# Four graph layers on one core: counts read in long runs, attention weights put ahead of their pieces, last rows stored bank by bank

## The chip, the cores and the metric

The kernel runs on one core of a Trainium2 chip. A core has TensorE (PE, matmuls and transposes), VectorE (DVE), ScalarE (ACT), GpSimd (POOL) and SyncE (SP); each works through its own list of instructions in order and waits for the others by semaphores. SP, POOL and ACT also issue DMAs. The metric is the device time of one execution in microseconds; the time before is the median of five runs.

## The reference

The input is a table of 3327 nodes with 512 features and an adjacency matrix of zeros and ones. Four layers follow one another, each as `x = layernorm(x + layer(x, adj))`:

```python
# layers 0, 2, 3: graph attention with 8, 8 and 4 heads
e = leaky_relu(f1[:, None] + f2[None, :])         # one number per pair of nodes and head
attention = softmax(where(adj > 0, e, -9e15))     # over the neighbours
h = attention @ (x @ W)                           # layers 2 and 3: elu of it
# layer 1: mean over the first 64 neighbours
keep = adj & (cumsum(adj, axis=1) <= 64)
cnt = keep.sum(axis=1)
xj = leaky_relu(((keep @ x) / max(cnt, 1)) @ W_nb.T + b_nb)
xi = leaky_relu(x @ W_line.T + b_line)
out = xi + where(cnt > 0, xj, 0)
```

## The kernel before

The nodes are padded to 26 tiles of 128 rows (`NT`), and a row of 512 floats is 2 KB. The mask is kept on the chip for the whole run, with one byte for each pair of nodes. Half of the nodes (`HALF`, 13 tiles) is attended to at a time.

**An attention layer** (`Layer`) first projects every tile: `project1` transposes a tile by four PE transposes into `pt`, ACT copies it to `xT` (L260), and `project2` makes two banks `pw` from it (L269), from which ACT takes the head columns `rc`, `qc`, `dc` (L270, L273) and DVE the values `vt` (L275). `prepare` turns the columns of one half into rows by PE transposes `pr` and ACT copies `rr` (L310, L312), and into scale and bias columns on DVE (L316 to L320). `cut` splits columns into bf16 pieces `pc` and copies them into `sden` and `sm`, the stationary operands of the denominators (L333 to L349). `attention` then runs two halves times four slices (`unit`). In each slice, for every source tile j, DVE makes the weights `t` (L403, 128x1664), ACT makes the corrections `y` from them (L406), and PE multiplies `t` with the values into `po` (L426); `den` adds the denominators in `pd` three tiles later (L378). Work of other kinds is put between the tiles as `jobs`, one after each tile.

After a slice, `transposed` (L454) brings the result back to rows by quads of tiles (`QUADS`: 4, 4, 4 and 1), and it is stored to `hd`. The denominators of the second half's last slice go through DRAM: `dd` is stored by one DMA (L505), and `place` (L515) reads it back as `pes` by 16 DMAs. These are held as `late` and run inside the next stage, at its loop's tiles 4 (`place`, on SP) and 8 (`finish_sums`, on DVE).

**Finishing a layer** (`finish_steps`) is done tile by tile inside the next stage's projection: load `h` and the residual `xr` (L126), divide by the denominators on DVE (L181), for layers with elu an exp on ACT (L186) and two additions on DVE (L192, L193), otherwise one (L195), and the layer norm (`norm_rows`: statistics on DVE L152, L153, a square root on ACT L154, reciprocal and shift on DVE L155, L158, the scaling on ACT L161). Loads of `h` go by SP or POOL, those of `xr` by POOL.

**The neighbour mean** (`sage`) projects each tile twice (`pz` L722, `pi` L725) and then sums over the kept neighbours (`acc` L845). The counts `cnt` of each node come from `ctd`, a DRAM tensor whose row 26 holds one count for each node. They are read by one DMA into `cb` (128 partitions, 26 columns, one bf16 element at a time: `"o (t p) -> p (o t)"`) and turned into three columns at the loop's tile 8.

**The third stage** (`third`) finishes layer 2 and projects layer 3. Its loop loads groups of two tiles ahead (`load_group`), and runs the steps of the group after the current one between the current tile's two projection steps.

**The tail.** Layer 3's first half is finished and stored inside the attention to the second (`later`). The second half stays in `g` on the chip; its last slice is finished by `final` after the last matmul: a division (L999), an exp (L1002), two additions (L1004, L1005) and statistics (L1008, L1009), for each quad in turn. Then the tiles are scaled in two groups, of 8 and 5 tiles, and stored, even tiles by SP and odd ones by POOL (`store`).

**What sets the order.** PE's list follows the program text (`manual_schedule`). The other engines' lists are made by a scheduler, which orders instructions by its own estimate of when each can run; `tc.keep_in_program_order(ins)` pins one instruction to its place in the program. So an edit can change the order of instructions around it, on DVE, ACT and SP alike, that the diff does not name. Tile pools with a number of buffers (`bufs`) make an instruction wait until a buffer's last reader is done.

## Time and profile before

| what | value |
|---|---|
| median of five runs | 3388.35 us (3386.66 to 3393.47) |
| the profiled execution's own time | 3390.44 us |
| its span, from the first instruction to the last | 3388.7 us |
| granted TensorE clock | 0.984 of full |
| instructions | 47192 |
| bytes moved by DMA | 284.29 MB, 84 GB/s on average |

The stages lie as follows in the trace: layer 0 until 958 us; the neighbour mean's projection 960 to 1170 and its sums to 1765; the second attention (layer 2) 1768 to 2556; the third stage's projection 2557 to 2696; the attention of layer 3 to 3359; the tail to 3388.7.

A line of the timeline gives the start, the time in us, the engine, the line in the kernel, the operation, output and inputs with their shapes, the number of instructions put together, and in brackets the time that the engine sat idle before it and what ended this. An "SPq" or "POOL" line with DMA_DIRECT2D is the issue of a transfer, not the transfer. The chain of waits is followed back from the last instruction, at each step to what released it.

### The profile page before, as it was taken

The numbers are of one execution on the slowest core, as the hardware profiler recorded it, in microseconds if no ns is written. First come the engines' busy times: TensorE is split into PE (matmuls) and PEld (weight loads), VectorE is DVE, ScalarE is ACT, GpSimd is POOL, SyncE is SP. The second block draws the span as 40 slices with busy tenths as digits, with TensorE's granted clock in tenths as the row PEclk, the third lists the DMA queues.
The fourth block names the chain that finished last, engine by engine and source line by source line (L and its number), as shares of the span: only waits on it lengthen the run. The fifth ranks groups of instructions, "written<-read, shape, count | busy, mean of one in ns | idle before, by whom it ended". The sixth has DMA issues, their size and how long they took to land.

```text
span 3388.7 us, 47192 instructions
## 1 busy us (share of the span) xinstructions
PE 3253.3 (96%) x18475; PEld 1626.1 (48%) x18475; DVE 2684.2 (79%) x2615; ACT 2357.0 (70%) x2142; POOL 241.7 (7%) x390
## 2 busy tenths in 40 slices
PE   8899999999979999999989999999998999999997
PEld 6634344444434445545544444444446754445443
DVE  5799999999967544444449999999998766668886
ACT  2398998999953333333338999999997755558985
POOL 3100000000010011111110000000002000010110
PEclk9999999999989999999999999999999999999998
DMA  9644111110143343333320111111117411122311
GB/s 369 221 128 124 49 49 40 57 45 28 44 122 122 115 128 85 88 84 87 82 77 19 48 50 48 50 50 42 38 33 234 159 41 42 41 51 78 97 42 49
DMA packets 288055, 284.29 MB, mean 84 GB/s; under 512 B 107533, under 2 KB 223575, under 8 KB 287832
## 3 DMA queue, kind: packets, MB, share of 16 engines
q1 hardware_dynamic: 254024, 170.61, 16.7%
q0 software_dynamic: 28288, 102.97, 9.6%
q10 hardware_dynamic: 5520, 7.69, 0.7%
q8 instruction: 146, 2.39, 0.3%
q14 instruction: 77, 0.63, 0.1%
HBM read 212.01 MB, written 69.17 MB: 83 GB/s over the span
## 4 chain that ended last, share of the span: by engine, by line
PE 83%; DVE 5%; DMA 5%; issue 4%; ACT 3%; POOL 0%; SPq 0%; ACTq 0%; POOLq 0%; DVEq 0%
PE po L426 49%; PE acc L845 12%; PE pd L378 7%; PE pw L269 5%; DVE t L403 3%; PE pz L722 3%; PE pi L725 3%; DMA raw<-in_adjT_dram 2%; ACT y L406 1%; PE pk L805 1%; PE pt L454 1%; DMA asb<-in_a_dram 0%; DMA r<-rr 0%; PE pa L1066 0%; PE pt L259 0%
## 5 line engine op out<-in xcount | busy, mean ns | idle before, releaser
L403 DVE SCALAR_TENSOR_TENSOR t<-rb,qc,mask 128x1664 f32<-128x1664 f32 x1040 | 1958.8, 1943 | 168.1 <-PE po L426 148.0
L406 ACT ACTIVATE y<-t,bi,sc 128x1664 fp8e4<-128x1664 f32 x1040 | 1769.5, 1765 | 309.9 <-PE pd L378 291.4
L426 PE MATMUL po<-t,vj 128*64 128x448 f32 (+3 forms) x8320 | 1909.8, 520 | 24.4 <-DVE t L403 24.1
L426 PEld LDWEIGHTS po<-t,vj 128*64 128x64 f32 (+1 forms) x8320 | 837.4, 148 | 974.5 <-issue 706.7
L845 PE MATMUL acc<-zs,kt 128*128 128x512 bf16 x1352 | 402.1, 381 | 0.0
L845 PEld LDWEIGHTS <-kt 128*128 128x128 fp8e4 x2002 | 196.5, 98 | 242.1 <-issue 8.4
L269 PE MATMUL pw<-wsb,xT 128*128 128x264 f32 (+1 forms) x1248 | 300.4, 396 | 12.3 <-DVE vt L275 10.0
L797 ACT CAST pk<-cy 128x512 f32<-128x512 bf16 x169 | 99.1, 588 | 278.0 <-DVE kt L809 268.1
L378 PE MATMUL pd<-y,sden 128*32 128x448 fp8e4 (+1 forms) x4160 | 259.3, 341 | 10.4 <-ACT y L406 10.4
L269 PEld LDWEIGHTS pw<-wsb,xT 128*128 128x128 f32 x1248 | 240.4, 196 | 57.0 <-ACT xT L260 10.4
L845 PE MATMUL acc<-zl,kt 128*128 128x512 bf16 x650 | 246.9, 380 | 0.0
L378 PEld LDWEIGHTS <-sden 128*32 128x32 bf16 x4160 | 117.3, 96 | 162.6 <-issue 139.8
L809 DVE SCALAR_TENSOR_TENSOR kt<-pk,mask 128x512 fp8e4<-128x512 f32 x169 | 116.0, 687 | 95.5 <-PE pk L805 95.5
L275 DVE TENSOR_TENSOR vt<-pw,dc 128x256 f32<-128x256 f32 x156 | 59.1, 417 | 150.6 <-ACT dc L270 144.8
L357 POOL DMA_DIRECT2D rb<-r x40 | 21.3, 532 | 1686.7 <-DVE t L403 1663.8
L273 ACT COPY rc<-pw 128x8 f32<-128x8 f32 (+1 forms) x78 | 12.7, 163 | 156.3 <-PE pw L269 156.3
L817 DVE SCALAR_TENSOR_TENSOR y<-acc,cnt,bnb 128x512 f32<-128x512 f32 x26 | 19.5, 750 | 97.5 <-PE acc L845 90.0
L690 POOL DMA_DIRECT2D cy<-ctd x91 | 67.9, 747 | 386.3 <-ACT pk L797 312.5
L722 PE MATMUL pz<-wn,xT 128*128 128x512 f32 x208 | 94.7, 598 | 0.4 <-ACT xT L716 0.4
L725 PE MATMUL pi<-wl,xT 128*128 128x512 f32 x208 | 93.5, 592 | 0.0
L154 ACT ACT_TABLE_LOAD x46 | 59.0, 1283 | 37.0 <-DVE mv L153 36.4
L624 DVE TENSOR_SCALAR mask<-raw 128x832 fp8e4<-128x832 int32 (+2 forms) x90 | 53.7, 604 | 38.8 <-DMA raw<-in_adjT_dram 38.6
(185 smaller groups left out, 1702.2 us busy)
## 6 DMA issues: line engine op xcount, KB each, us to landing
vj<-v SPq DMA_DIRECT2D x312, 128.0 KB
rb<-r POOLq DMA_DIRECT2D x40, 832.0 KB, 4.7
raw<-in_adjT_dram SPq DMA_DIRECT2D x67, 416.0 KB
cy<-ctd POOLq DMA_DIRECT2D x78, 256.0 KB, 4.0
h<-hd SPq DMA_DIRECT2D x61, 256.0 KB
v<-vt SPq DMA_DIRECT2D x50, 256.0 KB
hd<-hb SPq DMA_DIRECT2D x48, 256.0 KB
xr<-x POOLq DMA_DIRECT2D x45, 256.0 KB, 3.2
```

The lines of the kernel that those rows point to most:

```text
L269: nc.tensor.matmul(pw[e][:, :FW + H], xT[:, c, :], wsb[:, c, e, :], start=c == 0, stop=c == FC - 1)
L275: nc.vector.tensor_tensor(vt[:, hs, :], pw[e][:, :FW].rearrange("p (h d) -> p h d", d=D), self.dc[:, t, hs].rearrange("p (h e) -> p h e", e=1)
L378: nc.tensor.matmul(pd[c][32 * kk:32 * kk + 32, :w_], lhsT, rhs, start=(kk, c) not in seen, skip_group_check=final is not None, stop=last a ...
L403: nc.vector.scalar_tensor_tensor(t, rb[k], self.qc[:, j, h:h + 1], mask[:, j, i0:i0 + IW], op0=ALU.max, op1=ALU.mult)
L406: nc.scalar.activation(y, t, AF.Sigmoid, bias=self.bi[:, j, h:h + 1], scale=self.sc[:, j, h:h + 1], saturate=False)
L426: nc.tensor.matmul(po[c][k * D:(k + 1) * D, :z - a_], vj[:, j % 2, k * D:(k + 1) * D], ts[k][:, a_:z], start=j == 0, stop=j == NT - 1)
L690: nc.gpsimd.dma_start(out=cy[:, :n, :], in_=ctd[t:t + n, b * GW:(b + 1) * GW] .rearrange("(o t) i -> o t i", o=1).to_broadcast([P, n, GW]))
L722: nc.tensor.matmul(pz, xT[:, c, :], wn[:, c, :], start=c == 0, stop=c == FC - 1)
L725: nc.tensor.matmul(pi, xT[:, c, :], wl[:, c, :], start=c == 0, stop=c == FC - 1)
L797: nc.scalar.copy(pks[k % 2], carry[b, t // 4 * 4][:, t % 4:t % 4 + 2, :])
L809: nc.vector.scalar_tensor_tensor(kt, pk, NEIGHBOURS, mask[:, t:t + 2, i0:i0 + GW], op0=ALU.is_le, op1=ALU.mult, saturate=False)
L845: nc.tensor.matmul(acc, kts[t][:, s * P:(s + 1) * P], zs(t, c) if c < 2 else zl[:, t, :], start=t == 0 and c == 0, stop=t == NT - 1 and c ...
```

## The change

There are five edits, in three places of the program and two helpers that they share.

1. Counts. The row of counts is loaded as 26 rows of 128 elements (`cr`, by SP), copied to float by ACT (`cf`), transposed by PE at the loop's tile 8, and the three `cnt` operations read it from PSUM. The first of them is no longer pinned.
2. `place` pins the first of its 16 loads to its place in the program, where it runs in the next stage (layers 0 and 2).
3. `finish_steps` can pin the exp of a group's first tile; `load_group` asks for this for the group of tiles 2 and 3.
4. Second attention. `cut` of the first half moves from before the attention into its jobs, as the second one, with its first copy pinned. `prepare` and `cut` of the second half come two jobs later.
5. Tail. In the last slice all quads are divided first (quad k+2 is transposed after quad k is divided), with buffers of their own for the last two. Then come the four exps, and for each quad two additions, statistics and the square root, after which the quad before it is scaled and stored. All these are pinned in this order.

```diff
@@ finish_steps
+            pinned=False
             if layer.elu:
                 e = pool.tile([P, F], F32, name="e", bufs=ebufs)
-                nc.scalar.activation(e, h, AF.Exp)
+                ins = nc.scalar.activation(e, h, AF.Exp)
+                if pinned and s == 0:
+                    tc.keep_in_program_order(ins)
@@ place
                         for m in range(4):
-                            eng.dma_start(out=pes[...], in_=src[m])
+                            ins = eng.dma_start(out=pes[...], in_=src[m])
+                            if end and kk + m == 0:
+                                tc.keep_in_program_order(ins)
@@ unit, final
             take = []
-            return [lambda: take.append(transposed(*QUADS[0])), lambda: take.append(transposed(*QUADS[1])),
-                    sums, reciprocals] + [lambda q=q: take[q]() for q in range(2)] + \
-                [lambda q=q: transposed(*q)() for q in QUADS[2:]]
+            def step(k):
+                if k < len(QUADS):
+                    take.append(transposed(*QUADS[k]))
+            jobs = [lambda: step(0), lambda: step(1), sums, reciprocals]
+            for k in range(len(QUADS)):
+                jobs += [lambda k=k: take[k](), lambda k=k: step(k + 2)]
+            return jobs
@@ sage
-                cb = zp.tile([P, NT], BF, name="cb")
-                nc.gpsimd.dma_start(out=cb, in_=ctd[NT:NT + 1, :].rearrange("o (t p) -> p (o t)", p=P))
+                cr = fp.tile([NT, P], BF, name="cr", bufs=1)
+                nc.sync.dma_start(out=cr, in_=ctd[NT:NT + 1, :].rearrange("o (t p) -> (o t) p", p=P))
...
                     if t0 == 8:
-                        tc.keep_in_program_order(
-                            nc.vector.tensor_scalar(cnt[:, 0, :], cb, NEIGHBOURS, 1.0, op0=ALU.min, op1=ALU.max))
+                        cf = fp.tile([NT, P], F32, name="cf", bufs=1)
+                        nc.scalar.copy(cf, cr)
+                        pt = ps.tile([P, FC, P], F32, name="pt")
+                        cb = pt[:, 0, :NT]
+                        nc.tensor.transpose(cb, cf, ident[:NT, :NT])
+                        nc.vector.tensor_scalar(cnt[:, 0, :], cb, NEIGHBOURS, 1.0, op0=ALU.min, op1=ALU.max)
@@ third, load_group
-                        groups.append(finish_steps(fp, x2, L2, t0, 2, 10, nc.gpsimd if t0 < 4 else nc.sync, 6))
+                        groups.append(finish_steps(fp, x2, L2, t0, 2, 10, nc.gpsimd if t0 < 4 else nc.sync, 6,
+                                                    pinned=t0 == 2))
@@ third, final (divide, exp, add1, add2 are the former take() cut into functions)
+                def scale(q0, n):
+                    qs = slice(q0, q0 + n)
+                    keep(nc.vector.reciprocal(rs[:, qs, 0], rs[:, qs, 0]))
+                    keep(nc.vector.scalar_tensor_tensor(rs[:, qs, 1], mv[:, qs, 0], -1.0, rs[:, qs, 0], ...))
+                    for q in range(q0, q0 + n):
+                        y = g[:, q, :]
+                        if q % 4 == 3:
+                            keep(nc.scalar.activation(y, y, AF.Identity, bias=rs[:, q, 1:2], scale=rs[:, q, 0:1]))
+                        else:
+                            keep(nc.vector.tensor_scalar(y, y, rs[:, q, 0:1], rs[:, q, 1:2], ...))
+                        store(y, HALF + q, q)
+                for _, _, exp, _, _ in lasts:
+                    keep(exp())
+                for k, (q0, n, _, add1, add2) in enumerate(lasts):
+                    keep(add1())
+                    keep(add2())
+                    for q in range(q0, q0 + n):
+                        keep(nc.vector.bn_stats(out=st[:, q, 1, :], in_=g[:, q, FB:]))
+                        keep(nc.vector.bn_aggr(out=mv[:, q, :], in_=st[:, q, :, :]))
+                    keep(nc.scalar.activation(rs[:, q0:q0 + n, 0], mv[:, q0:q0 + n, 1], AF.Sqrt, bias=eps))
+                    if k > 0:
+                        scale(*lasts[k - 1][:2])
+                scale(*lasts[-1][:2])
@@ second attention
-                L2.cut(mp, 0, "pc", 1)
-                L2.attention(rp, lambda pool, half, s: [lambda: None] * 2 +
-                             [lambda: L2.prepare(mp, 1, "rr", 1, True), lambda: L2.cut(mp, 1, "pc", 1, True)]
+                L2.attention(rp, lambda pool, half, s: [lambda: None, lambda: L2.cut(mp, 0, "pc", 1, True)] +
+                             [lambda: None] * 2 + [lambda: L2.prepare(mp, 1, "rr", 1, True), lambda: L2.cut(mp, 1, "pc", 1, True)]
                              if (half, s) == (0, 0) else [],
```

## The prediction

> **What bounds the kernel now.** I read the page's busy shares and the shares of the chain of waits first, then the chain and the timelines of the four places that the change touches.
>
> ```profile
> PE 3253.3 (96%) x18475; PEld 1626.1 (48%) x18475; DVE 2684.2 (79%) x2615; ACT 2357.0 (70%) x2142; POOL 241.7 (7%) x390
> PE 83%; DVE 5%; DMA 5%; issue 4%; ACT 3%; POOL 0%; SPq 0%; ACTq 0%; POOLq 0%; DVEq 0%
> ```
>
> TensorE is busy 96% of the span: there is little to win outside its few gaps, and everything that only moves work beside it is free. One gap is where the neighbour mean starts (chain first, then the timelines of DVE and PE):
>
> ```profile
> 960.99 9.09 DMA dd<-red
> ...
> 979.46 3.19 DMA pes<-dd
> 968.56 0.18 DVE L753 TENSOR_SCALAR cnt<-cb 128x26 f32<-128x26 bf16 x1 [7.60 <-DMA cb<-ctd]
> 974.22 0.69 DVE L195 TENSOR_TENSOR h<-h,xr 128x512 f32<-128x512 f32 x1 [4.25 <-DMA xr<-in_x_dram]
> 980.87 0.69 DVE L181 TENSOR_TENSOR h<-h,rec 128x512 f32<-128x512 f32 x1 [3.23 <-DMA h<-hd]
> 986.31 1.12 PE L714 MATMUL pt<-ident,h 128*128 128x128 f32 x4 [17.00 <-ACT h L161]
> ```
>
> PE waits 17.00 us for tile 2, whose finish hangs on DVE, which waits in order for three loads. After it PE's timeline shows no wait until 1170, so what is won here stays won. The second attention is the opposite case; its start on PE, and a stretch of it by engine (length; PE, PEld, DVE, ACT and POOL busy; clock; DMA):
>
> ```profile
> 1770.11 1.06 PE L426 MATMUL po<-t,vj 128*64 128x448 f32 x2 [4.29 <-DVE t L403]
> 1773.84 10.48 PE L426 MATMUL po<-t,vj 128*64 128x448 f32 x46 [2.67 <-DVE t L403]
> 1968.00:2168.00 200.00, 199.12 (x1424) 93.66 (x1422) 200.00 (x108) 187.27 (x128) 2.65 (x5) 1.00 0.15 49
> ```
>
> DVE has 200.00 of 200 us there, so DVE sets its end. The third projection is mixed; its waits on DVE and PE:
>
> ```profile
> 2567.47 0.69 DVE L181 TENSOR_TENSOR h<-h,rec 128x512 f32<-128x512 f32 x1 [3.75 <-DMA h<-hd]
> 2575.91 1.12 PE L259 MATMUL pt<-ident,h 128*128 128x128 f32 x4 [6.63 <-ACT h L161]
> 2587.34 0.66 PE L259 MATMUL pt<-ident,h 128*128 128x128 f32 x4 [1.42 <-ACT h L161]
> 2637.81 1.23 PE L310 MATMUL pr<-ident,rc 128*4 128x128 f32 x5 [2.87 <-ACT rr L312]
> ```
>
> The tail after the last matmul is DVE, then transfers at full rate (last line, a window):
>
> ```profile
> 3365.80 1.29 DVE L1004 SCALAR_TENSOR_TENSOR g<-e,g 128x512 f32<-128x512 f32 x2
> 3368.72 0.24 DVE L1008 BATCH_NORM_STATS2 st<-g 128x6 f32<-128x128 f32 x1
> 3368.87 0.19 DVE L1009 BATCH_NORM_AGGREGATE mv<-st 128x2 f32<-128x12 f32 x1
> 3375.57 2.62 SPq L133 DMA_DIRECT2D out_dram<-g  x4
> 3378.16 1.92 DVE L1028 TENSOR_SCALAR g<-g,rs 128x512 f32<-128x512 f32 x4
> 3378.00:3386.00 8.00, 0.00 (x0) 0.00 (x0) 2.04 (x5) 0.81 (x1) 1.90 (x4) 0.50 1.01 353
> ```
>
> The profiled run took 3390.44 us (span 3388.7, 1.74 around it), 2.1 above the median 3388.35 and inside the runs' 3386.66 to 3393.47. I take the sum of differences from its rows and set it on the median.
>
> **A, the counts.** Removed: the load cb (POOL, 1.49 us to issue, 10.1 to landing) and DVE's wait for it. Added: cr, one SP issue (SP's loads take 0.32 to 0.5); a 26-column ACT copy (some 0.25 us) that stands before zs, where ACT waits anyway; one transpose (a group of four takes 1.12 us cold, 0.44 warm: 0.11); and cnt's reads from PSUM while PE is the bound. The wait of 7.60 by itself is worth only 0.7: behind it DVE waits for h until 969.27 and for xr until 974.22. What counts is the transfer. Windows of 2 us give 367 GB/s at 960 to 962, then 190 and 151 while cb's element-sized packets run: 682 of some 1440 KB, so 2.1 us are lost to all transfers. The store before xr and dd lie in that backlog, so both may come 2.1 earlier. SP then puts h(4) behind six pes issues instead of eight: 2 x 0.645 = 1.3. Against it, in the compiled order DVE adds tile 3 and the first projected rows after h(4)'s divide and not before, so h(4) to the last step of rs takes 5.7 us (nine passes of 0.6 and three short ones) and not 4.34: +1.4. Together -2.1 +1.4 -1.3 +0.1 = -1.9; tile 2's add is up to 0.6 sooner too, and I take **-2.2**. Ends: 0, if the 1 MB load of wl gates xr and not cb; -4, if both 2.1 and 1.3 count and DVE's 1.4 hides in a wait.
>
> **B, the second attention.** The first four t (1.864 us each, start to start) now precede the 19 cut operations, which took 1763.25 to 1768.13. PE's first product comes some 4 us earlier, but DVE has the same work and no idle time after, so it ends when it did. What is saved: operations that wait for their predecessor start 0.035 us after its end, others 0.08 before it; ten such waits x 0.115 = 1.2, some of which stay between neighbours: **-0.5**. Ends: -1.2; +0.3, if a t waits for its rows (rb 4.7 to landing, loaded long before). PE's transposes for the second half move two tiles later, under PE's own slack.
>
> **The third projection.** The edit is one pin on one exp, and a pin on the first of 16 pes issues, but the scheduler reorders DVE, ACT and SP. ACT now scales tiles 0 and 1 before the exp table load and the exp: first transposes 1.5 us earlier, worth nothing, because pw is in order and tile 2 is late. On DVE the work between the wait that ends at 2567.47 and rs of tile 2 was 7.4 us; now tiles 5 and 6 are divided first and tiles 4 and 5 added: 14 passes of 0.61, two halves of 0.33 and four short ones, 9.6: **+2.2** at the 6.63 wait. Tile 4 is then ready early, so the wait of 1.42 at 2587.34 goes: **-1.4**. At prepare, between the pr transposes and the copy that frees their bank, ACT has two table loads where it had one (1.28), and a sqrt, a dc and a wait for DVE in place of an exp: **+1.7** on the 2.87. Sum **+2.5**. Behind the moved DVE divide of tile 10 stand tile 7's add and a bank-freeing vt; its load is still behind the pes issues on SP (16 x 0.645), issued near 2582.5 and landing near 2586, when PE wants that bank at 2588.5: just hidden. Ends: -1.5 (only the stall that goes); +5.2, if 2.7 of that load are exposed.
> The Trainium skill, "ScalarE: Activation LUTs", What ACT_TABLE_LOAD costs, gives 1.28 us plus 1.38 us of drain for each switch. Here the load at 2633.85 is followed by exp at 2635.15, 1.30 later; no drain shows, and by the page the sum would be 1.4 higher.
>
> **C, the tail.** All four divides come first (the third waits for its transposes, about +0.65), then bank by bank add, add, statistics, with each step waiting for the one before. Rows: two adds of different banks start 0.605 apart; a dependent one would be 0.69 + 0.035 = 0.725. Statistics and aggregate interleaved cost 0.264 a tile (3368.72 to 3368.98), dependent 0.275 + 0.11 = 0.385. So +0.85 over the adds, +1.56 over 13 tiles, +0.82 for two more reciprocal and rs pairs, less 0.5 of waits for exp: DVE ends 3.4 later, at 3383.5. The first rows go out at 3374.1 instead of 3375.55, but after four of them DVE is away on bank 2 until 3378.9. Nine of 13 tiles, 2.36 MB, remain from about 3379.4 at 353 GB/s: 6.7 us, to 3386.1 against 3386.3. **-0.1**. Ends: -2.5, if dependent steps start as soon as independent ones do (0.605, 0.264), for then DVE keeps up and the transfers run unbroken from 3377; +1.5, if the last tile's two issues (0.73 each, after 3383.5) come last.
> The Trainium skill, "VectorE: DVE Perf Modes", The DRAIN you can't avoid, says that a semaphore between chained DVE operations costs nothing extra. By it C would be -2.5. The rows 3363.70, 3363.92 and 3364.14 (operations of 0.18, 0.216 apart, each waiting) against 0.605 for 0.69 speak against it.
>
> Sum: -2.2 - 0.5 + 2.5 - 0.1 = -0.3, so 3388.35 - 0.3 = **3388.0** (the profiled run's counterpart 3390.1).
>
> **The rivals.** Faster: the tail's transfers are what ends it, and they run unbroken: C at -2.5, and with A at -4 and B at -1.2 the third projection must give back under 1 to pass -6.8. For it speaks that DMA is the last thing running; against it the 0.605 and 0.725. Time 3381.0.
> Slower: the load of tile 10 that DVE waits for in order. Its neighbours took 2.9 to 8.5 us to landing; at 8.5 it lands at 2591, PE's bank comes 5 late and all of it lies on the path: -0.3 + 5 = 3393. It makes the change slower than before from 0.3 us of exposure on, and slower than can be told from no change from 7.
> The change doesn't do it: cb is not what delays xr and dd, since wl and blb (1.25 MB) are in the same backlog. Then A is 0 and the time 3390.2.
>
> **How the numbers follow.** This kernel can tell 0.2% (6.8 us) from no change. Likeliest case 0.52 (3384 to 3392), no gain from A 0.15, faster rival 0.19, slower 0.14. Past -6.8 lie 0.16 of the faster rival and 0.03 of the likeliest case: 0.19. Of the slower one 0.12 lies past +6.8, since the tail's +1.5 and A's 0 may join. The range 3380.5 to 3394.0 takes in both rivals' times and leaves out 2 in 10.
>
> **What would show it.** A: no wait for cb, xr's wait ending near 972, PE's 17.00 wait near 14.8. B: first t near 1764 on the old clock, and the attention still ending about where it did. Third projection: the first long PE wait longer than 6.63, the next one gone, a second table load before rr, and DVE waiting for h just before tile 7's add. C: statistics 0.385 apart, DVE's last operation later than before, a gap in the stores after the first four. I am wrong if DVE's waits there are not 0.035 behind the predecessor's end, if the reordered third projection costs more than 5, or if the earlier xr does not come.

## The result and the profile after

The changed kernel takes 3389.69 us (median of 26 runs, 3384.80 to 3397.24). The kernel before, run beside it on the same chips, takes 3392.85 us (44 runs, 3386.54 to 3399.02). The ratio is 0.9993, with a 95% interval of 0.9988 to 0.9998: 2.4 us less, between 4.1 and 0.7. By the bound of 0.2% that is no change. The profiled execution took 3389.86 us, with a span of 3388.1.

First the page's busy shares and the shares of the chain of waits, which hardly moved:

```profile
PE 3251.5 (96%) x18476; PEld 1625.8 (48%) x18476; DVE 2685.6 (79%) x2619; ACT 2353.5 (69%) x2143; POOL 240.3 (7%) x389
...
PE 83%; DVE 5%; DMA 4%; issue 4%; ACT 3%; POOL 0%; SPq 0%; ACTq 0%; POOLq 0%; DVEq 0%
```

The start of the neighbour mean, in the timelines of DVE and PE (start, time, engine, line, operation; in brackets the idle time before it and what ended it):

```profile
968.00 0.69 DVE L181 TENSOR_TENSOR h<-h,rec 128x512 f32<-128x512 f32 x1 [5.81 <-DMA h<-hd]
973.69 0.69 DVE L197 TENSOR_TENSOR h<-h,xr 128x512 f32<-128x512 f32 x1 [5.00 <-DMA xr<-in_x_dram]
977.82 0.69 DVE L181 TENSOR_TENSOR h<-h,rec 128x512 f32<-128x512 f32 x1 [2.02 <-DMA h<-hd]
...
984.57 1.12 PE L724 MATMUL pt<-ident,h 128*128 128x128 f32 x4 [14.04 <-ACT h L161]
```

The wait for `cb` is gone, and PE waits 14.04 us instead of 17.00. The windows of 2 us in which the packets of `cb` used to run (190 and 151 GB/s before) now move more:

```profile
964.00:966.00 2.00, 2.00 (x6) 0.88 (x5) 0.00 (x0) 0.00 (x0) 0.00 (x0) 1.00 0.95 289
966.00:968.00 2.00, 2.00 (x6) 0.95 (x5) 0.00 (x1) 0.00 (x0) 0.00 (x0) 1.00 1.11 337
```

The second attention starts 4.3 us earlier on DVE, counted from the last product of the projection before it (5.2 us by the two clocks). PE's first waits there are 2.43, now for the load of the values `vj`, and 2.07, where they were 4.29 and 2.67, and DVE is as full as before (the last line is the window of 200 us):

```profile
1762.97 5.67 DVE L405 SCALAR_TENSOR_TENSOR t<-rb,qc,mask 128x1664 f32<-128x1664 f32 x3
...
1767.41 0.94 PE L428 MATMUL po<-t,vj 128*64 128x448 f32 x2 [2.43 <-DMA vj<-v]
1780.72 3.01 PE L428 MATMUL po<-t,vj 128*64 128x448 f32 x14 [2.07 <-DVE t L405]
```
```profile
1968.00:2168.00 200.00, 199.12 (x1424) 93.54 (x1422) 200.00 (x108) 187.16 (x131) 2.12 (x4) 1.00 0.15 46
```

In the third projection the wait of 6.63 became 9.88, the 1.42 at tile 4 is gone, a wait of 1.29 stands where one of 2.00 stood, and 2.87 became 3.33:

```profile
2566.07 1.47 DVE L181 TENSOR_TENSOR h<-h,rec 128x512 f32<-128x512 f32 x2 [4.20 <-DMA h<-hd]
...
2576.70 1.11 PE L261 MATMUL pt<-ident,h 128*128 128x128 f32 x4 [9.88 <-ACT h L161]
2621.22 3.75 PE L271 MATMUL pw<-wsb,xT 128*128 128x260 f32 x16 [1.29 <-ACT xT L262]
2637.06 1.23 PE L312 MATMUL pr<-ident,rc 128*4 128x128 f32 x5 [3.33 <-ACT rr L314]
```

In the tail each statistic and its aggregate now cost 0.40 us a tile (3368.17 to 3368.57), and the last window moves 289 GB/s where it moved 353 (the first line is the first division):

```profile
3363.50 1.29 DVE L1019 TENSOR_TENSOR h<-pt,rec 128x512 f32<-128x512 f32 x2
...
3368.17 0.24 DVE L1066 BATCH_NORM_STATS2 st<-g 128x6 f32<-128x128 f32 x1
3368.44 0.21 DVE L1067 BATCH_NORM_AGGREGATE mv<-st 128x2 f32<-128x12 f32 x1
3368.57 0.24 DVE L1066 BATCH_NORM_STATS2 st<-g 128x6 f32<-128x128 f32 x1
...
3373.35 8.91 SPq L133 DMA_DIRECT2D out_dram<-g  x6
3382.20 0.55 DVE L1057 TENSOR_SCALAR g<-g,rs 128x512 f32<-128x512 f32 x1
```
```profile
3378.00:3386.00 8.00, 0.00 (x0) 0.00 (x0) 4.50 (x15) 1.47 (x3) 2.40 (x4) 0.50 0.81 289
```

### The profile page after: what moved, and what is told of

It is laid out like the page before. It is cut to its first block, busy times and chain, and to the rows that moved or that the text cites. A ratio compares the mean times of both kernels' runs of the same rounds, so it can differ in the third digit from the quotient of the medians.

```text
span 3388.1 us, 47182 instructions
## 1 busy us (share of the span) xinstructions
PE 3251.5 (96%) x18476; PEld 1625.8 (48%) x18476; DVE 2685.6 (79%) x2619; ACT 2353.5 (69%) x2143; POOL 240.3 (7%) x389
## 4 chain that ended last, share of the span: by engine, by line
PE 83%; DVE 5%; DMA 4%; issue 4%; ACT 3%; POOL 0%; SPq 0%; ACTq 0%; POOLq 0%; DVEq 0%
PE po L428 50%; PE acc L859 12%; PE pd L380 7%; PE pw L271 5%; DVE t L405 3%; PE pz L732 3%; PE pi L735 3%; DMA raw<-in_adjT_dram 3%; ACT y L408 1%; PE pk L819 1%; PE pt L456 1%; PE pa L1108 0%; DMA h<-hd 0%; PE pt L724 0%; PE pct L664 0%
```

## How the parts were measured

Each part is worth 0.5 to 3 us, and the interval of a run's ratio is about 3 us wide on either side of it. Stretches that no edit touches also differ from profile to profile: the neighbour sums took 570.6 to 573.5 us, the third attention 658.95 to 662.2. So each part is read in its own stretch of the profile, between two starts on the timeline:

- A: from the last `t` of layer 0 to the first product `acc` of the neighbour sums;
- B: from the last product of the projection for layer 2 to the last `t` of its attention;
- third: from that `t` to the last product `pw` of the third projection;
- C: from the tail's first division to the end of the span.

| kernel | ratio to before, 95% interval | A | B | third | C |
|---|---|---|---|---|---|
| before | 1 | 228.28 | 781.93 | 143.35 | 24.29 |
| changed | 0.9993 (0.9988 to 0.9998) | 225.71 | 780.94 | 144.05 | 24.62 |
| 1 counts alone | 1.0000 (0.9991 to 1.0009) | 227.12 | 780.92 | 142.97 | 24.73 |
| 2 cut alone | 0.9999 (0.9990 to 1.0008) | 228.33 | 780.84 | 143.72 | 25.47 |
| 3 cb twice | 1.0007 (0.9999 to 1.0016) | 230.38 | 781.86 | 143.05 | 24.68 |
| 4 tail alone | 1.0002 (0.9994 to 1.0011) | 228.42 | 780.91 | 143.47 | 25.61 |
| 5 changed, other order in the tail | 0.9989 (0.9980 to 0.9998) | 225.24 | 780.93 | 144.70 | 22.88 |
| 6 changed, pins in the third stage | 1.0023 (1.0013 to 1.0033) | 225.83 | 780.82 | 154.50 | 24.36 |
| 7 changed without the exp's pin | 0.9989 (0.9980 to 0.9998) | 225.74 | 780.64 | 143.54 | 24.77 |
| 8 as 6, pins in the neighbour mean too | 1.0019 (1.0010 to 1.0028) | 223.87 | 781.11 | 154.60 | 24.50 |
| 9 as 7, third stage ordered | 0.9987 (0.9978 to 0.9996) | 227.03 | 780.77 | 142.18 | 24.64 |
| 10 as 9, neighbour mean and tail too | 0.9977 (0.9967 to 0.9986) | 221.33 | 780.84 | 145.35 | 22.62 |
| 11 as 10, later divisions held back | 0.9976 (0.9967 to 0.9985) | 221.15 | 781.02 | 143.44 | 22.65 |
| 12 as 10, third stage left as in 7 | 0.9976 (0.9967 to 0.9986) | 221.38 | 780.89 | 143.89 | 22.51 |

Where a stretch is the same program in several rows, they show how far it repeats: A as before 228.28 to 228.42, third as before 142.97 to 143.89, B as before 780.91 to 781.93, C as before 24.29 to 25.47. Where A is as changed (changed kernel, runs 5, 6, 7 and 9) it spreads more, 225.24 to 227.03, and nearly all of this comes after PE's wait (last section). Up to PE's transposes of tile 2 the rows fall into two clear groups: 40.35 to 40.61 us in the three with `cb`'s load and the old program there, 37.25 to 37.77 in these five and in run 1.

## The experiments

### The parts one by one

**1. Counts alone.** The kernel before with only `cr`, `cf` and the transpose in place of `cb`.

```diff
-                cb = zp.tile([P, NT], BF, name="cb")
-                nc.gpsimd.dma_start(out=cb, in_=ctd[NT:NT + 1, :].rearrange("o (t p) -> p (o t)", p=P))
+                cr = fp.tile([NT, P], BF, name="cr", bufs=1)
+                nc.sync.dma_start(out=cr, in_=ctd[NT:NT + 1, :].rearrange("o (t p) -> (o t) p", p=P))
...
```

> The kernel before with the counts edit alone (part A). My theory: cb's element-sized packets take the transfers' time from dd, h and xr, so without them the neighbour mean's wait on PE for tile 2 falls from 17.00 to about 14.5 us (14.04 in the profile of the changed kernel), the wait for cb goes, and the first products after it (second tile's pz) come 2 to 3 us earlier relative to the stage's start. All later stages keep the order and the waits of before: third projection with 6.63 and 1.42, tail as before. Time: -2.2 us (0.9993). Rival 'the load of wl gates xr': wait stays within 0.5 of 17.00, time 0. Both are near what five rounds can tell, so the wait decides.

PE's wait fell to 14.09, as in the changed kernel. But stretch A gained only 1.2 us where the changed kernel gained 2.6. PE's timeline shows why: the same eight products took 6.17 us after the wait, and 4.70 in the changed kernel.

```profile
986.16 1.12 PE L714 MATMUL pt<-ident,h 128*128 128x128 f32 x4 [14.09 <-ACT h L161]
987.07 6.17 PE L722 MATMUL pz<-wn,xT 128*128 128x512 f32 x8
```

The windows of the first 4 us of these products (the last three columns are the granted clock, the DMA share and GB/s), first of this kernel, then of the changed one:

```profile
987.07:991.07 4.00, 4.00 (x6) 1.68 (x6) 4.00 (x11) 2.25 (x4) 0.97 (x2) 0.50 0.50 143
```
```profile
985.48:989.48 4.00, 4.00 (x8) 1.78 (x8) 3.93 (x11) 2.24 (x4) 0.88 (x2) 0.72 0.50 133
```

The granted clock was 0.50 in one and 0.72 in the other. So the edit wins 2.9 us at the wait, and the clock after the wait decides how much of it stays in one execution. That is not this kernel's doing: run 9 has the changed kernel's program in this stretch, and its eight products took 6.02 us and A 227.03. The pin on the loads of `place` (edit 2), which run 1 lacks, leaves no trace in this wait: 14.09 without it, 14.04 with it. The time (1.0000, within 0.09%) can't tell either from nothing.

**2. The cut's move alone.**

```diff
-                L2.cut(mp, 0, "pc", 1)
-                L2.attention(rp, lambda pool, half, s: [lambda: None] * 2 +
+                L2.attention(rp, lambda pool, half, s: [lambda: None, lambda: L2.cut(mp, 0, "pc", 1, True)] +
+                             [lambda: None] * 2 +
...
```

> The kernel before with the move of the first half's cut into the jobs of the second attention alone (part B). My theory: the first t starts 4 to 5 us earlier (before: 1768.13), PE's first product too, but DVE has the same work and no idle time, so the last t of the second attention comes only 0.5 to 1.0 us earlier than before, against the same kernel's last tile of the neighbour sums. Rival 'the earlier start is kept': the last t 4 to 5 us earlier, time -4 to -5 us (0.9987). Rival 'nothing at all': 0.

The first `t` came 1.64 us before the last product of the projection (as in the changed kernel) instead of 2.69 after it, so 4.3 us earlier. The last `t` came at 780.84 instead of 781.93. Over all kernels with this edit B has a mean of 780.88 (ten rows), over the four without it 781.41: -0.5, and no more is kept. This is DVE's 200.00 of 200. But the -0.5 is not the edit's alone. Of the four rows without it two stand at 781.9 and two at 780.9, with the same program, and the longer ones have a wait of DVE for PE that the others lack (0.75 in run 3; in the kernel before:)

```profile
1799.39 162.13 DVE L403 SCALAR_TENSOR_TENSOR t<-rb,qc,mask 128x1664 f32<-128x1664 f32 x87 [0.81 <-PE po L426]
```

Without DVE's idle time the four are at 780.8 to 781.0 and the ten at 780.6 to 780.7: the edit is worth about 0.2 us, and the rest is this wait, which comes and goes.

**3. The element-sized load twice.** The kernel before, with a second load of the counts into a tile that nobody reads.

```diff
+                cb2 = zp.tile([P, NT], BF, name="cb2")
+                nc.gpsimd.dma_start(out=cb2, in_=ctd[NT:NT + 1, :].rearrange("o (t p) -> p (o t)", p=P))
```

> The kernel before with the element-sized load of the counts made twice, the second into a tile that nobody reads; the rest as before, but POOL issues for 1.5 us more ahead of its load of tile 2, and SP puts one more 0.65 us issue ahead of tile 4's load. My theory for part A (the packets of cb take transfer time from all): xr's wait on DVE ends about 2 us later than in the kernel before, PE's wait grows from 17.00 to 19 to 19.7, time +2 to +2.7 us (1.0007). Rival 'the load of wl gates xr': PE's wait stays under 17.7, time +0 to +0.7. Rival 'only POOL's issue time counts': 18.5, +1.5.

```profile
971.22 0.69 DVE L181 TENSOR_TENSOR h<-h,rec 128x512 f32<-128x512 f32 x1 [3.89 <-DMA h<-hd]
975.93 0.69 DVE L195 TENSOR_TENSOR h<-h,xr 128x512 f32<-128x512 f32 x1 [4.02 <-DMA xr<-in_x_dram]
980.76 0.69 DVE L181 TENSOR_TENSOR h<-h,rec 128x512 f32<-128x512 f32 x1 [1.40 <-DMA h<-hd]
...
986.20 1.11 PE L714 MATMUL pt<-ident,h 128*128 128x128 f32 x4 [18.07 <-ACT h L161]
```

Layer 0's last `t` started at 944.54 here, at 945.70 in the kernel before and at 946.96 in the changed one. After it, the three waits of DVE ended like this:

| ends after layer 0's last t | no cb (changed) | cb once (before) | cb twice |
|---|---|---|---|
| h of tile 2 | 21.04 | 23.57 | 26.68 |
| xr of tile 2 | 26.73 | 28.52 | 31.39 |
| h of tile 4 | 30.86 | 35.17 | 36.22 |
| PE's transposes of tile 2 | 37.61 | 40.61 | 41.66 |

The cleanest witness is the store `dd`, which SP issues and POOL's list doesn't touch. The steps of the chain of waits (start, time) give its landing without `cb` (changed kernel), and with `cb` twice; it is 9.09 with one `cb`, and 7.04 in run 1. In runs 5, 6, 7 and 9, without `cb`, it is 6.93 to 7.30, and with one `cb` in runs 2 and 4 9.01 and 8.81:

```profile
962.21 7.31 DMA dd<-red
```
```profile
959.80 11.91 DMA dd<-red
```

So one element-sized load costs the transfers beside it 1.8 to 2.1 us and a second one 2.8, as the lost 2.1 us said. `wl` is in all four kernels, so the rival that it alone sets these times is out, and so is "only POOL's issue time", for `dd`. For `xr` the two can't be told apart cleanly: it lands 3.3 us after its issue in all three, and what moves is POOL's issue, which stands idle 10 us and more before it (10.45 before, 11.54 here) without a row that names what holds it.

PE's wait grew by 1.07 and not by 2, because what PE waits for in the end is `h` of tile 4, the last load that DVE waits for in order, and the second `cb` moved this by 1.05 only. Stretch A grew by 2.10; the rest is the clock after the wait (0.50).

**4. The tail alone.** The kernel before with the tail of the changed kernel (all of edit 5).

> The kernel before with the tail's new order alone (part C). My theory: DVE ends about 3.4 us later against the last slice's first division than before, the first rows go out 1.5 to 2 us earlier, the transfers stop for about 2 us after four or six rows, and the end stays where it was: -0.1 us, between -0.5 and +0.5 against the first division. Rival 'transfers unbroken': the end 2.5 us earlier. Rival 'the last tile's issues come last': +1.5 us.

DVE's last operation came 19.25 us after the first division (15.66 before), the first store 9.85 (11.16 before), as in the changed kernel. C is 24.75 on the mean of the six kernels with this tail and 24.79 on the mean of the four with the old one; single rows spread by 1.2. Any cost is below what these rows can tell.

**7. Without the exp's pin.**

```diff
-                ins = nc.scalar.activation(e, h, AF.Exp)
-                if pinned and s == 0:
-                    tc.keep_in_program_order(ins)
+                nc.scalar.activation(e, h, AF.Exp)
```

> The changed kernel without the pin on the exp of tile 2 in the third stage, all else as changed. My theory: this pin alone makes the scheduler reorder DVE and ACT in the third projection; without it the waits of before come back (6.63 for tile 2, 1.42 at tile 4, 2.87 at prepare instead of 9.88, none, 3.33). By my prediction's sum for this stage (+2.5) the kernel would be 2.5 us faster than the changed one; by the two profiles' marks (the third projection cost 0.7 us more from its first to its last product) only 0.7. Rival: the pin on the loads of place does it: then 9.88 stays and the time is the changed kernel's.

```profile
2568.88 1.11 PE L259 MATMUL pt<-ident,h 128*128 128x128 f32 x4 [7.09 <-ACT h L161]
2580.10 0.66 PE L259 MATMUL pt<-ident,h 128*128 128x128 f32 x4 [1.42 <-ACT h L161]
```

The waits of before came back, and the pin on the loads of `place` is still there, so the pin on one exp is what reorders this stage. The seven kernels with the old order have a mean of 143.43 in the third stretch, the two with the pinned one 144.05 and 144.70: the pin costs 0.95 us on the mean, and not 2.5. With only two rows on one side, and 0.9 between the lowest and the highest on the other, this is a size to within half a us or so; the changed kernel and run 7 alone differ by 0.5.

### Why tile 2 is late, and what that is worth

**6. Pins on the divisions of tiles 4 to 7, third stage.**

```diff
+            if layer is L2 and t0 in (4, 6):
+                tc.keep_in_program_order(ins)     # ins: the division, L181
```

> The changed kernel with the divisions of tiles 4 to 7 in the third stage pinned to their places in the program, so that DVE finishes tiles 2 and 3 before it waits in order for tile 4's load. Theory: what PE waits for with 9.88 us is not tile 2's own data but DVE's in-order wait for h of tile 4 (4.20, until 2566.07) and the four divisions and two additions put ahead; with them behind, tile 2 is finished about 7 us earlier, the 9.88 falls to 2 to 4, a wait of up to 3 us comes back at tile 4, and the time falls by 4 to 7 us (0.9982). Rival 'tile 2 is late by its own loads or by the exp table': the wait stays above 8 and the time within 1 us of the changed kernel. Rival 'the delay is only moved': tile 4 or 6 waits for what tile 2 wins, time 0 to -1.

```profile
2572.41 0.69 DVE L181 TENSOR_TENSOR h<-h,rec 128x512 f32<-128x512 f32 x1 [2.81 <-DMA h<-hd]
2574.43 0.69 DVE L181 TENSOR_TENSOR h<-h,rec 128x512 f32<-128x512 f32 x1 [1.33 <-DMA h<-hd]
...
2575.24 0.16 DVE L158 SCALAR_TENSOR_TENSOR rs<-mv,rs 128x2 f32<-128x2 f32 x1
...
2590.81 1.12 PE L263 MATMUL pt<-ident,h 128*128 128x128 f32 x4 [4.92 <-ACT h L161]
```

The expectation was wrong by its sign: 0.23% slower. The divisions of tiles 8 and 9, which were not pinned, were put ahead of L158 of tiles 2 and 3, and DVE waited there for their loads until 2574.43, though the aggregates were done at 2569.3. And a pinned division had to follow `xsum` (a sum that DVE takes over a tile's transposed copy) of a tile that PE had yet to transpose, so each pair was begun only when the one before it was done (4.92, 4.72). The same in-order wait, further on in the list, with more to lose.

**8. The same pins in the neighbour mean too** (`layer is not L3`).

> As the run before it, and the same two pins in the neighbour mean's projection (tiles 4 to 7), where DVE also waits in order for tile 4's load (until 977.82) before it ends tile 2, for which PE waits 14.04. Theory: tile 2 needs xr (973.69), one more addition, statistics, root and scale, so PE goes on near 979.5 instead of 984.57: the 14.04 falls to 9 to 10, and what tile 4 then waits is 0 to 2; with the third stage's gain the time falls by 7 to 11 us against the changed kernel (0.997). Rival 'only moved': the wait falls, but later waits take it back, and the time is that of the run with the third stage's pins alone.

There the wait fell from 14.04 to 11.36, not to the 9 to 10 expected, and A by 1.8 against the changed kernel; three operations of 2 us for tile 0 (`xi`) still stood ahead of L158. The time did not fall by 7 to 11 us but was 0.19% above the kernel before, because the third stage lost 10 us as in run 6.

**9. An order without pins.** A division is only told to stand behind one given instruction. The edit in short:

```diff
+            with tc.issue_after(L158 of tiles 2 and 3):     # tiles 4 to 7; 8 to 11 behind that of 4 and 5
+                the division, L181
...
+            with tc.issue_after(the scaling of tiles t + 2, t + 3):     # ACT, t = 0, 2, 4
+                the corrections dc of tile t
```

> The changed kernel without the pin on the exp, and with an order of issue (no waits, only places in the lists) in the third stage: on DVE the divisions of tiles 4 to 7 stand behind the last step of tiles 2 and 3 (L158), those of 8 to 11 behind the last step of tiles 4 and 5; on ACT the corrections dc of tiles 0, 2 and 4 stand behind the scaling of the two tiles finished meanwhile. It repeats the question of the run with pins on tiles 4 to 7, whose divisions of tiles 8 and 9 had slipped ahead of L158 and waited there for their loads. Theory (DVE's in-order wait for later tiles' h makes tile 2 late): PE's wait for tile 2, 7.09 without the exp's pin and 9.88 with it, falls to 2 to 4, the 1.42 goes, no wait over 3 us comes in their place, and the third projection is 4 to 6 us shorter: 0.9982 of the kernel before. Rival 'tile 2 is bound by its own loads, exp and tables': the wait stays above 6 and the time that of the changed kernel without the pin (0.9989). Rival 'only moved': tile 4 or 6 takes the gain back.

```profile
2565.76 0.66 PE L278 MATMUL pt<-ident,h 128*128 128x128 f32 x4 [0.71 <-ACT h L161]
2577.10 0.66 PE L278 MATMUL pt<-ident,h 128*128 128x128 f32 x4 [3.22 <-ACT h L161]
2597.63 0.66 PE L278 MATMUL pt<-ident,h 128*128 128x128 f32 x4 [2.53 <-ACT h L161]
```

The wait for tile 2 fell from 7.09 to 0.71. DVE's last step for tile 2 (L158) now starts at 2564.70, with no wait for a load ahead of it. So it was mostly DVE's in-order wait that made tile 2 late, and not its own loads or the exp table. The transposes came 6.4 us earlier after layer 2's last `t`. ACT's new order has a share in this that was not run alone: in run 7 the corrections and their table load (1.28 us) stand between the root and the scaling of tile 2, here behind it. I estimate it, from that load's time, at 1.3 us at most. But the stretch is only 1.4 us shorter than in run 7: waits of 3.22, 0.94, 2.53 and 1.21 came in its place. Both the theory and "only moved" hold, each for its half.

**10. The neighbour mean and the tail as well.** There the divisions of tiles 4 to 7 and the first operation of `xi` of tile 0 stand behind L158 of tiles 2 and 3; the tail has run 5's order, and ACT scales every second tile.

> As the run before it, and two more: in the neighbour mean's projection the divisions of tiles 4 to 7 and the first bias addition of tile 0 (L744) stand behind the last step of tiles 2 and 3 on DVE; and the tail has DVE's order with fewer dependent neighbours, and ACT scales every second tile instead of every fourth. Theory: the neighbour mean's wait falls from 14.04 to about 10 (xr lands at 973.7, then 5 us of steps); the tail ends 2 to 3 us earlier against its first division (DVE's end 3 us earlier, transfers then at their rate); with the third stage 8 to 12 us in all, 0.997 of the kernel before. Rival 'the transfers bound the tail': its end moves by no more than 1.5. Rival 'only moved' for the neighbour mean: less than 1 us between the last product of layer 0 and the sums.

A fell to 221.33, 4.4 below the changed kernel, with a wait of 9.29 instead of 14.04: nothing was only moved there:

```profile
981.12 1.12 PE L748 MATMUL pt<-ident,h 128*128 128x128 f32 x4 [9.29 <-ACT h L161]
```

In the third stage a wait that is 1.92 in run 9 was 6.69 here, with the same order of DVE's list:

```profile
2627.25 0.69 DVE L188 TENSOR_TENSOR h<-h,rec 128x512 f32<-128x512 f32 x1 [3.90 <-DMA h<-hd]
2629.92 0.69 DVE L188 TENSOR_TENSOR h<-h,rec 128x512 f32<-128x512 f32 x1 [1.98 <-DMA h<-hd]
...
2634.09 1.87 PE L336 MATMUL pr<-ident,rc 128*4 128x128 f32 x8 [6.69 <-ACT rc L299]
```

These are divisions that the scheduler puts several tiles ahead; in run 9 the same two waited 1.59 and 0.74. Why their loads landed later here, no run shows.

**11 and 12. Holding the later divisions back, and leaving the third stage alone.**

```diff
+    # 11: every pair from tile 8 on: its division behind L158 of the pair two pairs before
+    # 12: as run 10, without any issue_after in the third stage
```

> As the run with all three reorderings before it, but in the third stage every pair's division from tile 8 on stands on DVE behind the last step (L158) of the pair two pairs before it. Theory: the 6.69 at prepare in that run came from divisions put up to eight tiles ahead, where DVE waited in order for their h (3.90 and 1.98, until 2629.92); held back, these waits go, the 6.69 falls below 3 and the third projection is 3 us shorter or more: from the last t of layer 2 to the last product 141 to 142.5 us instead of 145.35, the time 2 to 4 us less (0.997 of the kernel before). Rival 'DVE's own work bounds this stage': the waits move to the finish of the pairs and the projection takes 144 or more.

> The changed kernel without the exp's pin, with the new orders in the neighbour mean and the tail, and with the third stage left as the scheduler makes it (waits 7.09 and 1.42 as in the run without the exp's pin). Theory: the neighbour mean is 4 to 4.7 us shorter than in the changed kernel, the tail 1.7 to 2, the third projection at 143 to 143.7 instead of 144.05: 6 to 7 us less than the changed kernel, 0.9975 of the kernel before. Rival 'the third stage's order is worth its 6 us': this run is slower than the one beside it by more than 3 us.

In run 11 DVE's waits for `h` late in the stage are gone and the 6.69 fell to 4.16, not below 3, and the stretch to 143.44 instead of 145.35: between its two theories. Run 12, with the scheduler's own order there, has 143.89 and the same time. The two medians are 3384.15 and 3384.12 us, against 3392.72 for the kernel before on the same chip. So all of the gain over run 7 lies in the neighbour mean and the tail, and the third stage's order is worth nothing measurable. Run 12 is the simplest kernel that beats both: 0.9976 of before (8 us), where the changed kernel has 0.9993.

### What dependence costs on DVE

**5. The tail's operations in another order.**

```diff
+                keep(lasts[0][3]())                       # the first bank's first addition
                 for k, (q0, n, _, add1, add2) in enumerate(lasts):
-                    keep(add1())
+                    if k + 1 < len(lasts):
+                        keep(lasts[k + 1][3]())           # the next bank's first addition
                     keep(add2())
-                    for q in range(q0, q0 + n):
-                        keep(nc.vector.bn_stats(out=st[:, q, 1, :], in_=g[:, q, FB:]))
-                        keep(nc.vector.bn_aggr(out=mv[:, q, :], in_=st[:, q, :, :]))
+                    for q in range(q0, q0 + n + 1):
+                        if q < q0 + n:
+                            keep(nc.vector.bn_stats(out=st[:, q, 1, :], in_=g[:, q, FB:]))
+                        if q > q0:
+                            keep(nc.vector.bn_aggr(out=mv[:, q - 1, :], in_=st[:, q - 1, :, :]))
```

> The changed kernel with the same operations in the tail, but on DVE the first addition of a bank stands before the second addition of the bank before it, and a tile's aggregate after the next tile's statistics, so that fewer operations follow the one they wait for. My theory (a dependent DVE operation starts 0.035 us after the end of the one before, an independent one 0.08 before it): statistics cost 0.26 to 0.30 a tile instead of 0.40, DVE's last operation comes 1.5 to 2 us earlier against the first division than in the changed kernel, the gap in the stores shrinks, and the end comes 0 to 1.5 us earlier, as the transfers then set it. Rival 'dependence costs nothing and the time lies in the operations themselves': DVE ends where it did, within 0.3.

```profile
3363.12 1.29 DVE L1019 TENSOR_TENSOR h<-pt,rec 128x512 f32<-128x512 f32 x2
...
3368.32 0.24 DVE L1069 BATCH_NORM_STATS2 st<-g 128x6 f32<-128x128 f32 x1
3368.48 0.19 DVE L1071 BATCH_NORM_AGGREGATE mv<-st 128x2 f32<-128x12 f32 x1
3368.59 0.24 DVE L1069 BATCH_NORM_STATS2 st<-g 128x6 f32<-128x128 f32 x1
...
3379.89 0.55 DVE L1057 TENSOR_SCALAR g<-g,rs 128x512 f32<-128x512 f32 x1
```

The same pair of operations costs 0.27 us here (3368.32 to 3368.59) and 0.40 in the changed kernel. DVE ends 17.31 us after the first division instead of 19.25, and C is 22.88 instead of 24.75 on the mean. The end gained as much as DVE did, 1.9 us, more than the 0 to 1.5 expected: in the changed kernel it was still DVE that set when the later stores could begin. C repeats to about 1.2 us only, but the four rows with this order (22.51 to 22.88) lie clear of the ten others (24.29 to 25.61). With one scaling fewer for each bank of four on DVE (runs 10 to 12) DVE ends at 15.97, another 1.3 earlier, and the end moves by 0.2 to 0.4 only, so from there on DVE no longer sets it; the transfers are what is left.

The Trainium skill, "VectorE: DVE Perf Modes", The DRAIN you can't avoid, says, from eight copies in a chain, that a semaphore between DVE operations costs nothing extra. In this case it doesn't hold: in run 5 the same operations, ordered so that fewer wait for their neighbour, take 1.9 us less. What a waiting neighbour pays for, the semaphore itself or something beside it, no run here separates.

## Why the prediction was right, point by point

The predicted 3388.0 us stood 0.3 below the median of five runs; the measured difference is 2.4 us (0.7 to 4.1), and both say "no change by 0.2%". The predicted difference itself lies just outside the measured interval. With 44 runs the kernel before has 3392.85 and not the 3388.35 of five, so the level was taken 4.5 too low; the changed kernel's 3389.69 is 1.7 above the number and inside the range. That the number came so near is partly luck: the low level and a sum that gave the change 2 us too little partly cancel. By stretches the parts sum to -2.6 (A) - 0.5 (B) + 0.95 (third) - 0.04 (C) = -2.2, against -2.2 - 0.5 + 2.5 - 0.1.

- **A**: -2.2 predicted, -2.6 in the stretch. Its steps, against layer 0's last `t`: `h` of tile 4 earlier by 4.3 (predicted 2.1 + 1.3), the steps from there to PE longer by 1.31 (6.75 instead of 5.44; predicted 1.4), so PE starts 3.0 earlier. The transfers of `cb` were the cause (run 3: `dd` lands in 7.3, 9.1 and 11.9 us); "A does nothing" is out. Of the 4.3, 1.8 is the earlier `dd` and 1.3 the two issues fewer, as worked out; the other 1.2 is that the load took 4.3 us from its issue and not 5.5, which the sum had not. What the working also lacked is the clock after the wait, worth up to 1.6.
- **B**: -0.5 predicted, -0.5 measured, but the match is luck: without DVE's waits for PE the edit is worth 0.2. PE's earlier start went where the text said, into DVE's full list. It was 1.9 us and not "some 4", because the first product then waited for `vj`.
- **Third**: the term that was mis-sized, +2.5 predicted, +0.95 measured. DVE's work between the wait and L158 of tile 2 took 9.57 us (7.4 before): the +2.2 was right, and PE's transposes of tile 2 came 2.6 later after the last `t`. The stall at tile 4 went, as predicted. The +1.7 at prepare was wrong: the second table load stands there, yet the wait grew by 0.46 only, as the first of the two loads began at 2631.96, 0.74 before PE's transposes `pr` at 2632.70. After both loads the next operation starts 1.29 to 1.30 us behind the load's own start (2633.57 to 2634.86 for the second), as the working took it. And two earlier waits of 0.65 and 2.00 gave way to 0.41 and 1.29, which the working had not looked at. In the pair of profiles the terms are +2.6 - 1.4 + 0.5 - 1.0 = +0.7, against +2.2 - 1.4 + 1.7 = +2.5.
- **The load of tile 10** stayed hidden in the changed kernel (DVE waited 1.17 for it). Its mechanism, and about its price of 5, showed elsewhere: the 6.69 in run 10.
- **C**: -0.1 predicted, -0.04 measured. Statistics at 0.40 a tile (predicted 0.385), DVE's end 3.6 later (3.4), first store 1.3 earlier (1.45), the transfers slack after the first stores (225 and 289 GB/s). In single profiles C is 24.29 and 24.62, and rows of one program differ by 1.2, so the -0.04 is no sharper than that. The working's picture held: the transfers pause while DVE is away on the second bank (94 GB/s from 3377.5 to 3379.5) and then run at 338, 343 and 315 GB/s in the next three windows of 2 us. The pause is DVE's doing, and its length carries over to the end: run 5 made DVE faster, and the end came 1.9 us earlier, inside the -2.5 that the working gave for a DVE that keeps up.

## What to carry to other kernels

An engine that works through its list in order is held by the load that stands next in the list, not by the one that the waiting engine needs: look for divisions and copies of later tiles ahead of the last step of the tile that is awaited, and put them behind that step. In the two places here a gain at one such wait stayed where DVE had room behind it (neighbour mean, run 10: DVE busy 123 of 180 us) and mostly came back as several small waits where it had little (third projection, run 9: 73 of 82 us). And where single parts are worth less than the runs can tell, read each in its own stretch of the profile and compare it with kernels in which that stretch is unchanged.

## What was not expected of the hardware

After PE's wait in the neighbour mean the first eight products of 128x512 took 4.59 to 4.78 us in six of the fourteen traces and 5.16 to 6.17 in the other eight. The granted clock is 0.50 at first and then 1.00, and the difference is when it changes. That doesn't go by the length of the wait: 14.04 and 17.00 gave the fast start, 14.09 and 18.07 the slow one. The traces agree on what it goes by. In each of them all changes of the granted clock lie whole multiples of 3.41 us apart, to 0.003 us. Where PE's transposes of tile 2 fell within 0.52 us of the start of such a step (six traces), the clock rose at the end of that step, 2.9 to 3.3 us after them; where they fell 0.75 us or more into it (eight traces), it rose only at the end of the next one, 4.0 to 6.1 us after them. Two windows of the kernel before, around its change at 989.20, and two of run 1, around 992.23 (the clock is third from the end):

```profile
986.31:989.19 2.88, 2.88 (x7) 1.85 (x8) 2.88 (x9) 1.54 (x3) 0.54 (x1) 0.50 0.68 219
989.21:993.00 3.79, 3.79 (x10) 1.64 (x10) 2.97 (x9) 2.14 (x4) 1.08 (x2) 1.00 0.45 125
```
```profile
986.16:992.22 6.06, 6.06 (x11) 2.96 (x12) 5.64 (x16) 3.35 (x6) 1.55 (x3) 0.50 0.57 172
992.24:995.00 2.76, 2.76 (x8) 1.30 (x7) 0.95 (x3) 2.38 (x4) 0.00 (x0) 1.00 0.21 83
```

So it is chance for one execution, and worth up to 1.6 us here, as much as a part of this change.

Reading 26 x 128 bf16 one element at a time, 6.7 KB in all, cost a store in flight beside it about 1.8 us (8.81 to 9.09 instead of 6.93 to 7.31), and a second such load 2.8 more.
